# Mamba block of a four-layer graph network: chunks of 1, 2, 3, 4, 4, ... tiles, the graph convolution shared out by TensorE's load per slot, and gates, projections and exponentials in other slots

## The chip, the cores and the metric

One core of a Trainium2 chip runs the whole program. The time is the device time of one execution in microseconds (us), the median of several executions; the same kernel before the change is the base.

## The reference

Four layers work on 3327 rows of 256 numbers with a dense 3327 x 3327 matrix `adj`; each layer's result is added to its input and normalised by row. The change is all in the second layer, which is a graph convolution followed by a selective scan ("Mamba"):

```python
h = relu(adj @ x @ gcn_w + gcn_b)
h = layernorm(h) * ln_g + ln_b
xc, z = split(h @ w_in)                       # 512 channels each
u = silu(causal_conv4(xc) + conv_b)
dt_low, B, C = split(u @ w_xp)                # 16, 16 and 16 columns
dt = softplus(dt_low @ w_dt + b_dt)
# along the rows, for each of 512 channels and 16 states s:
state[s] = exp(dt * A[s]) * state[s] + dt * B[s] * u
y = sum_s(state[s] * C[s]) + u * D_skip
x = layernorm(x + (y * silu(z)) @ w_out)
```

The other layers are a graph layer (`adj @ x / degree`), a graph attention and a two-step nucleus attention. Their code is the same in both kernels.

## The kernel before

Rows are padded to 26 tiles of 128. A *chunk* is a run of tiles that the scan takes at once; before, the chunks have 2, 2, 3, 3, 4, 4, 4 and 4 tiles (list `ends`). Inside a chunk the kernel goes over the 16 states; one state of one chunk is a *slot*, written (c,s) here, and there are 128 of them. Channels lie on partitions in four groups `g`, rows along the free axis.

In slot k the engines do this, in the order of the loop over `states`:

- SP fetches the row pair (B, C) of slot k+2, broadcast over the partitions (`row`, three buffers).
- PE adds up the product of slot k-1 into PSUM by transposes (`add_up`).
- DVE does four scans (`scan`, one per group). Each needs `dA`, an exponential that ACT writes into one of two PSUM buffers (`decay`); ACT writes the third and fourth of this slot and the first two of the next one, each as soon as a scan has freed a buffer. Then DVE multiplies by C (`product`).
- ACT saves the last column (`carry`).
- POOL multiplies `du` by the B row of slot k+2 (`feed`), into the buffer that `product` has just read.
- After that come the slot's `uses`: on PE and ACT, work of the neighbouring chunks. For the chunk behind: `gated` and `residual` (slots 1 to 4) turn and project its output. For this chunk: `gate_input`. For the next chunk, the methods of class `Head`: `project` (which begins with a POOL copy of three columns, `t<-last`), `taps`, `silu`, `mixed`, `step_size`, `exponentials`, `logarithms`, `finish`, `skip`.
- Between the uses, `work_ahead` draws pieces of the graph convolution of later tiles from the generator `convolve`. A tile is 26 matmuls into one PSUM buffer `cb`, then a boundary: ACT copies `m`, PE transposes, ACT copies again, PE multiplies by `gcn_w`, ACT does the relu (`hn<-cb`), and only then is `cb` free. Three later steps (`measure`, `norm`, `turn`) normalise the tile and turn it into `hT`.

Before, a piece is 6 matmuls (`JM`), `quota` counts pieces and spreads them evenly in rows over the 16 slots, and half of a slot's pieces come between its first and its other uses. When all tiles are convolved, `work_ahead` calls `values`, which prepares the third layer's input tile by tile, as far as `ready` allows.

All these PSUM results of the uses share one buffer `ps`. From `pinned = True` on, class `Ordered` keeps every engine's instructions in the order in which the code issues them; they all have the line of that helper, L263. What stands before that point (the first tiles and the first `Head`) is ordered by the scheduler. So within an engine an instruction that waits holds up all that stand behind it.

Of the kernel before, what the change touches and what calls it, by code (L numbers as in the profile page):

```python
# [18 lines left out]
P = 128  # L19
# [2 lines left out]
JH = 13  # L22
J0 = 4
JC = 9
JM = 6
NS = 7
S0 = 5
WC = 512
DI = 512
NG = DI // P  # L30
# [16 lines left out]
def gnn_kernel(ctx: ExitStack, tc: tile.TileContext, n: int, a: dict, out: bass.AP):  # L47
# [109 lines left out]
    with tc.tile_pool(name="l1b", bufs=1) as wpool, tc.tile_pool(name="l1at", bufs=2) as l1at:  # L157
# [33 lines left out]
        with tc.tile_pool(name="l1aw", bufs=1) as cwork, tc.tile_pool(name="l1c", bufs=2) as ch, \  # L191
# [6 lines left out]
            def scratch():  # L198
                return tmp.tile([P, NG, 3 + WC], F32, name="t")
# [45 lines left out]
            ends = []  # L245
            while not ends or ends[-1] < npad:
                prev = ends[-1] if ends else 0
                ends.append(min(npad, prev + min(WC, (2 + len(ends) // 2) * P)))
            nch = len(ends)
            starts = [0] + ends[:-1]  # L250
            hTs, us, szs, rows_of = {}, {}, {}, {}
# [25 lines left out]
            def convolve():  # L277

                rest = []
                full = 0  # L280
                for it in range(nt):
                    cb = cpsum.tile([P, 2, D], F32, name="cb")
                    acc, tp = cb[:, 0, :], cb[:, 1, :]
                    for j in range(nt):
                        if j % JC == 0:
                            m = min(JC, nt - j)
                            at = l1at.tile([P, JC, P], F32, name="at")
                            nc.sync.dma_start(at[:, :m, :], a["adjT"][it][:, j:j + m, :])
                        ten.matmul(acc, at[:, j % JC, :], X0[:, j, :], start=(j == 0), stop=(j == nt - 1))
                        if j % JM == JM - 1 and j < nt - 1:  # L290
                            if rest:
                                rest.pop(0)()
                            yield full
                    m = cwork.tile([P, D], F32, name="m")
                    act.copy(m, acc)
                    while rest:
                        step = rest.pop(0)
                        step()
                        full += step is turn
                    yield full  # L300
                    for k in range(2):
                        ten.transpose(tp[:, k * P:(k + 1) * P], m[:, k * P:(k + 1) * P], ident)
                    mt = cwork.tile([P, D], F32, name="m")
                    act.copy(mt, tp)
                    yield full
# [4 lines left out]
                    act.activation(h, acc, AF.Relu)  # L310
# [12 lines left out]

                    def turn(it=it, h=h):
                        c = next(x for x in range(nch) if it * P < ends[x])
                        i = it * P - starts[c]
                        if i == 0:
                            hTs[c] = ch.tile([P, D // P, WC], F32, name="hT", bufs=3)
                        pt = psum.tile([P, WC], F32, name="ps")
                        for k in range(2):  # L330
                            ten.transpose(pt[:, k * P:(k + 1) * P], h[:, k * P:(k + 1) * P], ident)
                        for k in range(2):
                            act.activation(hTs[c][:, k, i:i + P], pt[:, k * P:(k + 1) * P], AF.Identity,
                                                 scale=g1[:, k:k + 1], bias=b1[:, k:k + 1])
                    rest = [lambda: None, measure, lambda: None, lambda: None, norm, turn]
                    while it == 0 and rest:
                        rest.pop(0)()
                    full += it == 0
                    yield full
                for step in rest[1:]:  # L340
                    step()
                    full += step is turn
                    yield full

            stream = convolve()
            done = taken = 0
# [2 lines left out]
            def advance():  # L349

                nonlocal done, taken
                t = next(stream, None)
                if t is not None:
                    done, taken = t, taken + 1
                return t is not None

            def pump(tiles):

                while done < min(tiles, nt) and advance():
                    pass  # L360

            def quota(c, s):


                c, s = divmod(c * DS + s + DS - S0, DS)
                t0 = ends[c] if c < nch else npad
                t1 = ends[c + 1] if c + 1 < nch else npad + P
                return max(0, math.ceil(NS * (t0 + (t1 - t0) * (s + 1) / DS) / P + NS - 1 - taken))

            def work_ahead(steps):  # L370

                for _ in range(steps):
                    if not advance():
                        return values()

            def value(it):

# [25 lines left out]
            class Head:  # L403
# [52 lines left out]
                    act.activation(self.v[:, g, :], ps[:, :w], AF.Identity, bias=b_dt[:, g:g + 1])  # L456
                    act.activation(self.e[:, g, :], ps[:, :w], AF.Abs, bias=b_dt[:, g:g + 1])

                def exponentials(self):

                    e = self.e
                    act.activation(e, e, AF.Exp, scale=-1.0)
                    self.e1 = scratch()[:, :, :self.w]
                    act.activation(self.e1, e, AF.Identity, bias=1.0)

                def logarithms(self):

# [106 lines left out]
                gps.tensor_scalar(nb, nb, -1.0, None, op0=ALU.mult)  # L574
                return rs, nb

            def tiles_of(c):
                return (ends[c] - starts[c]) // P

            pump(ends[0] // P)  # L580
            xs, ys = {}, {}
            first = Head(0)
            with tc.high_priority():
                for g in range(NG):
                    first.project(g)
                    first.taps(g)
            work_ahead(2)
            with tc.high_priority():
                first.silu()
                first.mixed()  # L590
            work_ahead(2)
            with tc.high_priority():
                for g in range(NG):
                    first.step_size(g)
            work_ahead(2)
            with tc.high_priority():
                first.exponentials()
                first.logarithms()
                first.finish()
                first.skip()  # L600
            states = [(c, s) for c in range(nch) for s in range(DS)]
            rows = {k: row(k) for k in range(2)}
            for k in range(2):
# [4 lines left out]
            for k, (c, s) in enumerate(states):  # L608
# [49 lines left out]
                if c and 1 <= s <= tiles_of(c - 1):  # L658
# [5 lines left out]
                    def projected(c=c, s=s, plus=plus, sums=sums):  # L664
                        sums[s] = residual(c - 1, s - 1, plus["gt"])
                    uses += [turned, projected]
                if s in (7, 8):
                    uses += [lambda i=i: gate_input(c, i) for i in range(2 * (s - 7), min(m, 2 * (s - 6)))]
                if after:
                    if s in (5, 6):  # L670
                        if s == S0:
                            pump(ends[c + 1] // P)
                        uses += [lambda g=g: ahead.project(g) for g in (2 * s - 10, 2 * s - 9)]
                    if s == 10:
                        uses += [ahead.mixed]
                    uses += [lambda g=g: ahead.step_size(g) for g in {10: (0,), 11: (1, 2), 12: (3,)}.get(s, ())]
                    if s == 12:
                        uses += [ahead.exponentials]
                    if s == 15:
                        uses += [ahead.skip]  # L680
                if c and s in (7, 8):
                    for i in range(2 * (s - 7), min(tiles_of(c - 1), 2 * (s - 6))):
                        x = X[:, starts[c - 1] // P + i, :]
                        rs, nb = plus["scales"]
                        act.activation(x, x, AF.Identity, scale=rs[:, i:i + 1], bias=nb[:, i:i + 1])
                    if s == 8:
                        ready = ends[c - 1] // P
# [835 lines left out]
```

## Time and profile before

| | us |
|---|---|
| median of three runs (3743.65 to 3745.7) | 3745.27 |
| the profiled execution: its time | 3741.57 |
| its span in the profile | 3739.6 |
| first layer and first convolved tiles, up to the first scan | 433.26 |
| slots (0,0) to (7,15), first scan to last scan | 1154.17 |
| of these, DVE busy | 898 |
| last scan to the third layer's start | 27.47 |

Times inside the profile are counted from the start of the span. The first scan of a slot marks its start. DVE's scans are the instructions `h<-dA,...`; `cb<-F,at` is a convolution matmul, which is two instructions on PE; `y<-ident,hc` is `add_up`. The granted clock is a share of TensorE's full clock.

### The profile page before, as it was taken

How to read it: one execution, taken by the hardware profiler on the slowest of the kernel's cores; microseconds unless marked ns; L12 is line 12 of the kernel's file. 1: busy time of each engine (PE TensorE's matmuls, PEld its weight loads, DVE VectorE, ACT ScalarE, POOL GpSimd, SP SyncE). 2: the span in 40 equal slices, each digit the busy share in tenths (PEclk: the TensorE clock that was granted, in tenths of full speed). 3: DMA queues.
4: the chain of work that ended last, by engine and by line, in shares of the span. 5: the costliest groups of instructions: out<-in, count | busy, mean ns of one | idle time of the engine just before them, and what ended most of it. 6: DMA issues, size and time to landing. Idle time of an engine off the chain costs nothing. (4 is left out here: it accounts for less than half of the span.)

```text
span 3739.6 us, 43358 instructions
## 1 busy us (share of the span) xinstructions
PE 3301.6 (88%) x15583; PEld 2604.1 (70%) x15583; DVE 2418.5 (65%) x5460; ACT 1705.0 (46%) x2594; POOL 903.5 (24%) x970
## 2 busy tenths in 40 slices
PE   9999787877877766589989999999999899999996
PEld 7888565665655645478876787787777677777775
DVE  1111377777888878867755445445442899999996
ACT  1000456455454555421113333333333888888883
POOL 0000143443544444511110000000000233333332
PEclk9999888888989887799999999999999999999998
DMA  7442333332323211234432221121121212222220
GB/s 243 138 138 97 93 92 85 89 96 79 105 86 87 77 48 51 51 118 144 151 109 60 63 61 53 57 63 52 56 64 53 65 56 66 66 66 66 66 62 22
DMA packets 151996, 308.01 MB, mean 82 GB/s; under 512 B 19859, under 2 KB 77395, under 8 KB 151635
## 3 DMA queue, kind: packets, MB, share of 16 engines
q1 hardware_dynamic: 151762, 305.06, 27.3%
q8 instruction: 126, 2.06, 0.2%
q14 instruction: 108, 0.88, 0.1%
HBM read 294.36 MB, written 10.65 MB: 82 GB/s over the span
## 5 line engine op out<-in xcount | busy, mean ns | idle before, releaser
L263 POOL TENSOR_TENSOR h<-du,row 128x2048 f32<-128x2048 f32 (+2 forms) x126 | 470.0, 3730 | 615.1 <-DVE hc L263 463.6
L263 DVE TENSOR_TENSOR_SCAN h<-dA,carry,h 128x512 f32<-128x512 f32 (+2 forms) x448 | 480.9, 1115 | 179.2 <-ACT dA L263 179.2
L263 ACT ACTIVATE dA<-t,A_log 128x512 f32<-128x512 f32 (+2 forms) x510 | 305.3, 609 | 276.8 <-DVE h L263 274.3
L263 PE MATMUL cb<-F,at 128*128 128x256 f32 x1148 | 296.4, 411 | 69.4 <-ACT hn L263 69.1
L966 PE MATMUL acc<-F,at 128*128 128x256 f32 x1352 | 352.5, 386 | 1.0 <-ACT q L740 0.6
L999 PE MATMUL acc<-X,wt 128*128 128x256 f32 x1352 | 343.6, 391 | 10.6 <-ACT wt L997 10.2
L999 PE MATMUL acc<-G,wt 128*128 128x256 f32 x1352 | 334.2, 390 | 5.7 <-ACT wt L930 5.3
L263 PE MATMUL y<-ident,hc 128*128 128x128 f32 x1648 | 253.3, 316 | 83.0 <-DVE hc L263 82.7
L263 PEld LDWEIGHTS cb<-F,at 128*128 128x128 f32 x1148 | 232.3, 207 | 133.0 <-ACT hn L263 77.2
L999 PEld LDWEIGHTS acc<-X,wt 128*128 128x128 f32 x1352 | 242.7, 190 | 105.3 <-issue 41.3
L119 PE MATMUL acc<-xa,at 128*128 128x257 f32 x1352 | 308.5, 381 | 5.9 <-DMA at<-in_adjT 5.7
L966 PE MATMUL acc<-X,at 128*128 128x256 f32 x1352 | 308.4, 381 | 0.0
L263 PEld LDWEIGHTS y<-ident,hc 128*128 128x128 f32 x1648 | 231.4, 166 | 110.1 <-DVE hc L263 97.1
L875 PE MATMUL acc<-F,at 128*128 128x257 f32 x1352 | 303.7, 381 | 1.1 <-ACT r L848 1.1
L999 PEld LDWEIGHTS acc<-G,wt 128*128 128x128 f32 x1352 | 248.8, 192 | 64.3 <-ACT wt L930 34.9
L1011 DVE MAX8 cand<-e 128x8 f32<-128x128 f32 x676 | 142.3, 279 | 228.8 <-ACT e L952 217.2
L966 PEld LDWEIGHTS acc<-F,at 128*128 128x128 f32 x1352 | 237.1, 190 | 74.9 <-issue 50.2
L119 PEld LDWEIGHTS acc<-xa,at 128*128 128x128 f32 x1352 | 255.6, 191 | 42.8 <-issue 6.2
L966 PEld LDWEIGHTS acc<-X,at 128*128 128x128 f32 x1352 | 253.0, 191 | 39.9 <-issue 8.0
L875 PEld LDWEIGHTS acc<-F,at 128*128 128x128 f32 x1352 | 253.6, 191 | 36.7 <-issue 1.3
L263 DVE TENSOR_TENSOR hc<-h,row 128x2048 f32<-128x2048 f32 (+2 forms) x128 | 243.7, 1904 | 10.3 <-PE y L263 4.2
L995 PE MATMUL tp<-ident,e 128*128 128x128 f32 x1352 | 196.6, 277 | 43.1 <-DVE e L1182 35.1
(361 smaller groups left out, 5150.7 us busy)
## 6 DMA issues: line engine op xcount, KB each, us to landing
at<-in_adjT SPq DMA_DIRECT2D x102, 832.0 KB, 4.4
at<-in_adjT SPq DMA_DIRECT2D x260, 320.0 KB, 2.9
row<-bc SPq DMA_DIRECT2D x64, 512.0 KB, 4.9
at<-in_adjT SPq DMA_DIRECT2D x52, 576.0 KB, 3.8
at<-in_adjT SPq DMA_DIRECT2D x26, 512.0 KB, 4.0
row<-bc SPq DMA_DIRECT2D x32, 384.0 KB, 4.8
row<-bc SPq DMA_DIRECT2D x32, 256.0 KB, 4.8
xt<-in_xT SPq DMA_DIRECT2D x26, 128.0 KB, 4.0
```

What stands on the lines that cost most here:

```text
L119: nc.tensor.matmul(acc, at[:, j, :], rhs[:, j0 + j, :], start=(j0 + j == 0), stop=(j0 + j == nt - 1))
L263: return lambda *x, **k: tc.keep_in_program_order(op(*x, **k))
L875: nc.tensor.matmul(acc, at[:, j, :], F[:, j0 + j, :], start=(j0 + j == 0), stop=(j0 + j == nt - 1))
L966: nc.tensor.matmul(acc, at[:, j, :], rhs[:, j0 + j, :], start=(j0 + j == 0), stop=(j0 + j == nt - 1))
L995: nc.tensor.transpose(pt[:, j, :], e[:, (j0 + j) * P:(j0 + j + 1) * P], ident)
L999: nc.tensor.matmul(acc, wt[:, j, :], rhs[:, j0 + j, :], start=(j0 + j == 0), stop=(j0 + j == nt - 1))
L1011: nc.vector.max(cand[:, s * 8:(s + 1) * 8], z[:, s * SEG:(s + 1) * SEG])
```

## The change

The chunks become 1, 2, 3, 4, 4, 4, 4 and 4 tiles. Convolution pieces become 3 matmuls, and each piece tells its load in units (4 for a 256-column matmul, so 122 for a tile with its boundary). `duty` gives the units that a slot's other work puts on PE, and `quota` fills the slots from slot 7 of one chunk to slot 6 of the next up to a common level, with a lead of `AHEAD` = 96 units. Between the first and the second use stands only what `SPLIT` leaves. `norm` and `turn` come two pieces later. The projections move from slots 5, 6 to slots 7, 8, the gates' inputs from 7, 8 to 5, 6, the taps from 7 (groups 0, 1), 8 (2) and 9 (3) to 8 (0, 1) and 9 (2, 3); the first half of the exponentials from slot 12 to slot 11; the scaling of the finished rows `X`, and with it `ready`, from slots 7, 8 to slot 14. Two tiles more than the first chunk are convolved before the loop.

```diff
-JM = 6
-NS = 7
-S0 = 5
+JM = 3
+TILE = 122
+AHEAD = 96
+SPLIT = 54
+S0 = 7
...
-                ends.append(min(npad, prev + min(WC, (2 + len(ends) // 2) * P)))
+                ends.append(min(npad, prev + min(WC, (1 + len(ends)) * P)))
...
                         if j % JM == JM - 1 and j < nt - 1:
                             if rest:
-                                rest.pop(0)()
-                            yield full
+                                step = rest.pop(0)
+                                step()
+                                full += step is turn
+                            yield full, 4 * JM
...
-                    rest = [lambda: None, measure, lambda: None, lambda: None, norm, turn]
-                    while it == 0 and rest:
-                        rest.pop(0)()
-                    full += it == 0
-                    yield full
+                    rest = [lambda: None, measure, *3 * [lambda: None], norm, lambda: None, turn]
+                    if not pinned:
+                        for step in (measure, norm, turn):
+                            step()
+                        rest = []
+                        full += 1
+                    yield full, 14
...
+            def duty(c, s):
+                if c >= nch:
+                    return 0
+                m, n, b = tiles_of(c), tiles_of(c + 1), tiles_of(c - 1)
+                return 4 * m * (2 if s == 0 else 1) + 20 * (1 <= s <= b) + 16 * len(gates(s, m)) \
+                    + 4 * n * len(projects(s)) + (8 * n if s == 10 else 0) + 2 * n * len(sizes(s))
...
             def quota(c, s):
                 c, s = divmod(c * DS + s + DS - S0, DS)
-                t0 = ends[c] if c < nch else npad
-                t1 = ends[c + 1] if c + 1 < nch else npad + P
-                return max(0, math.ceil(NS * (t0 + (t1 - t0) * (s + 1) / DS) / P + NS - 1 - taken))
+                if c not in shares:
+                    slots = [divmod((c - 1) * DS + S0 + i, DS) for i in range(DS)]
+                    busy = [duty(*x) for x in slots]
+                    more = TILE * tiles_of(c + 1)
+                    level = max(busy) + more
+                    while sum(max(0, level - x) for x in busy) > more:
+                        level -= 1
+                    shares[c] = [max(0, level - x) for x in busy]
+                target = TILE * ends[c] // P + sum(shares[c][:s + 1]) if c + 1 < nch else TILE * nt
+                return target + AHEAD - taken
...
-                def exponentials(self):
-                    e = self.e
+                def exponentials(self, g):
+                    e = self.e[:, g:g + 2, :]
                     act.activation(e, e, AF.Exp, scale=-1.0)
-                    self.e1 = scratch()[:, :, :self.w]
-                    act.activation(self.e1, e, AF.Identity, bias=1.0)
+                    if g:
+                        self.e1 = scratch()[:, :, :self.w]
+                        act.activation(self.e1, self.e, AF.Identity, bias=1.0)
...
-            work_ahead(2)
...
                 first.skip()
+            pump(ends[1] // P)
...
-                    for g in {7: (0, 1), 8: (2,), 9: (3,)}.get(s, ()):
+                    for g in {8: (0, 1), 9: (2, 3)}.get(s, ()):
                         ahead.taps(g)
...
-                if s in (7, 8):
-                    uses += [lambda i=i: gate_input(c, i) for i in range(2 * (s - 7), min(m, 2 * (s - 6)))]
+                uses += [lambda i=i: gate_input(c, i) for i in gates(s, m)]
                 if after:
-                    if s in (5, 6):
-                        if s == S0:
-                            pump(ends[c + 1] // P)
-                        uses += [lambda g=g: ahead.project(g) for g in (2 * s - 10, 2 * s - 9)]
+                    if s == S0:
+                        pump(ends[c + 1] // P)
+                    uses += [lambda g=g: ahead.project(g) for g in projects(s)]
...
-                    if s == 12:
-                        uses += [ahead.exponentials]
+                    if s in (11, 12):
+                        uses += [lambda: ahead.exponentials(2 * (s - 11))]
...
-                if c and s in (7, 8):
-                    for i in range(2 * (s - 7), min(tiles_of(c - 1), 2 * (s - 6))):
+                if c and s == 14:
+                    rs, nb = plus["scales"]
+                    for i in range(tiles_of(c - 1)):
...
-                q = quota(c, s) if done < nt else 2
+                q = quota(c, s)
+                if done == nt:
+                    for use in uses[:1]:
+                        use()
+                    values()
+                    for use in uses[1:]:
+                        use()
+                    values()
+                    continue
+                part = min(q, max(0, SPLIT - 4 * m - duty(c, s) // 2)) if len(uses) > 1 else q
                 for use in uses[:1]:
                     use()
-                work_ahead((q + 1) // 2)
+                work_ahead(part)
                 for use in uses[1:]:
                     use()
-                work_ahead(q // 2)
+                work_ahead(quota(c, s))
```

More of the change, by code (lines that the diff above doesn't have):

```diff
@@ L291, in convolve @@
                             if rest:
-                                rest.pop(0)()
-                            yield full
+                                step = rest.pop(0)
+                                step()
+                                full += step is turn
+                            yield full, 4 * JM
                     m = cwork.tile([P, D], F32, name="m")
                     act.copy(m, acc)
[L296 to L299, printed above, removed]
-                    yield full
+                    yield full, 8
                     for k in range(2):
@@ L304, in convolve @@
                     act.copy(mt, tp)
-                    yield full
+                    yield full, 4
                     for k in range(2):
@@ L334, in turn @@
                                                  scale=g1[:, k:k + 1], bias=b1[:, k:k + 1])
-                    rest = [lambda: None, measure, lambda: None, lambda: None, norm, turn]
-                    while it == 0 and rest:
-                        rest.pop(0)()
-                    full += it == 0
-                    yield full
+                    rest = [lambda: None, measure, *3 * [lambda: None], norm, lambda: None, turn]
[5 more added lines that the diff above has]
+                    yield full, 14
                 for step in rest[1:]:
@@ L342, in convolve @@
                     full += step is turn
-                    yield full
+                    yield full, 0
             stream = convolve()
@@ L353, in advance @@
                 if t is not None:
-                    done, taken = t, taken + 1
+                    done, taken = t[0], taken + t[1]
                 return t is not None
@@ L360, in pump, with tiles_of, gates, projects @@
                     pass
+            def duty(c, s):
[4 more added lines that the diff above has]
+                    + 4 * n * len(projects(s)) + (8 * n if s == 10 else 0) + 2 * n * len(sizes(s))
+            def tiles_of(c):
+                return (ends[c] - starts[c]) // P if 0 <= c < nch else 0
+            def gates(s, m):
+                return range(2 * (s - 5), min(m, 2 * (s - 4))) if s in (5, 6) else ()
+            def projects(s):
+                return range(2 * (s - S0), 2 * (s - S0) + 2) if s in (S0, S0 + 1) else ()
+            def sizes(s):
+                return {10: (0,), 11: (1, 2), 12: (3,)}.get(s, ())
+            shares = {}
             def quota(c, s):
                 c, s = divmod(c * DS + s + DS - S0, DS)
-                t0 = ends[c] if c < nch else npad
-                t1 = ends[c + 1] if c + 1 < nch else npad + P
-                return max(0, math.ceil(NS * (t0 + (t1 - t0) * (s + 1) / DS) / P + NS - 1 - taken))
-            def work_ahead(steps):
-                for _ in range(steps):
+                if c not in shares:
[8 more added lines that the diff above has]
+                return target + AHEAD - taken
+            def work_ahead(units):
+                while units > 0:
+                    before = taken
                     if not advance():
                         return values()
+                    units -= max(1, taken - before)
             def value(it):
@@ L575, in scales @@
                 return rs, nb
-            def tiles_of(c):
-                return (ends[c] - starts[c]) // P
             pump(ends[0] // P)
@@ L586, in gnn_kernel @@
                     first.taps(g)
-            work_ahead(2)
-            with tc.high_priority():
                 first.silu()
                 first.mixed()
-            work_ahead(2)
-            with tc.high_priority():
                 for g in range(NG):
                     first.step_size(g)
-            work_ahead(2)
-            with tc.high_priority():
-                first.exponentials()
+                for g in (0, 2):
+                    first.exponentials(g)
                 first.logarithms()
@@ L674, in gnn_kernel @@
                     if s == 10:
                         uses += [ahead.mixed]
-                    uses += [lambda g=g: ahead.step_size(g) for g in {10: (0,), 11: (1, 2), 12: (3,)}.get(s, ())]
-                    if s == 12:
-                        uses += [ahead.exponentials]
+                    uses += [lambda g=g: ahead.step_size(g) for g in sizes(s)]
+                    if s in (11, 12):
+                        uses += [lambda: ahead.exponentials(2 * (s - 11))]
                     if s == 15:
@@ L680, in gnn_kernel @@
                         uses += [ahead.skip]
-                if c and s in (7, 8):
-                    for i in range(2 * (s - 7), min(tiles_of(c - 1), 2 * (s - 6))):
+                if c and s == 14:
+                    rs, nb = plus["scales"]
+                    for i in range(tiles_of(c - 1)):
                         x = X[:, starts[c - 1] // P + i, :]
-                        rs, nb = plus["scales"]
                         act.activation(x, x, AF.Identity, scale=rs[:, i:i + 1], bias=nb[:, i:i + 1])
-                    if s == 8:
-                        ready = ends[c - 1] // P
@@ L688, in gnn_kernel @@
-                q = quota(c, s) if done < nt else 2
+                    ready = ends[c - 1] // P
+                q = quota(c, s)
[8 more added lines that the diff above has]
+                part = min(q, max(0, SPLIT - 4 * m - duty(c, s) // 2)) if len(uses) > 1 else q
                 for use in uses[:1]:
```

## Prediction

> **What bounds the kernel now.** I read the busy table by stretches first: one stretch from first scan to first scan of each chunk. Columns are length, then busy us of PE, PEld, DVE, ACT, POOL, the granted clock, DMA.
>
> ```profile
> 433.26:537.12 103.86, 81.09 (x361) 62.67 (x359) 70.71 (x102) 58.72 (x133) 41.83 (x27) 0.85 0.36 93
> 787.51:940.60 153.09, 119.82 (x532) 90.95 (x532) 111.63 (x118) 78.53 (x144) 62.78 (x33) 0.87 0.33 89
> 940.60:1108.81 168.21, 129.12 (x600) 99.17 (x600) 136.76 (x118) 86.40 (x146) 80.96 (x37) 0.88 0.32 93
> 1446.29:1587.43 141.14, 86.48 (x400) 69.22 (x400) 117.05 (x96) 66.84 (x138) 71.33 (x19) 0.78 0.21 52
> ```
>
> DVE is the fullest engine but idles 24 to 41 us in every chunk, whatever its size: 898 busy in 1154, so 256 us idle. The change can win only there, or before the first scan. Second, DVE's waits from 433 to 1587:
>
> ```profile
> DVE h L263 <- ACT dA L263: 201.0, 74, 7.2
> DVE X L263 <- PE ps L263: 28.4, 18, 3.4
> DVE sz L263 <- PE y L263: 6.0, 6, 1.8
> ```
>
> Four fifths is scans waiting for `dA`. ACT itself is half idle; it is late because its queue is in order and the uses in front of `dA` wait. Third, the timeline shows on what, in slots (4,5) and (4,6):
>
> ```profile
> 992.58 1.99 PE L263 MATMUL ps<-hT,w_in 128*128 128x512 f32 x4
> 992.77 2.45 DVE L263 TENSOR_TENSOR_SCAN h<-dA,carry,h 128x512 f32<-128x512 f32 x2
> 992.99 4.50 POOL L263 TENSOR_TENSOR h<-du,row 128x2048 f32<-128x2048 f32 x1 [2.58 <-DVE hc L263]
> 997.43 0.20 POOL L263 COPY t<-last 128x12 f32<-128x12 f32 x1
> 997.66 0.81 ACT L263 ACTIVATE u<-t,conv_b,conv_w 128x512 f32<-128x512 f32 x1 [5.86 <-POOL t L263]
> 998.38 0.36 ACT L263 ACTIVATE hn<-cb 128x256 f32<-128x256 f32 x1
> 998.64 0.58 ACT L263 COPY t<-ps 128x512 f32<-128x512 f32 x1
> 999.97 1.28 ACT L263 ACTIVATE dA<-t,A_log 128x512 f32<-128x512 f32 x2
> 1000.68 1.28 DVE L263 TENSOR_TENSOR_SCAN h<-dA,carry,h 128x512 f32<-128x512 f32 x1 [5.45 <-ACT dA L263]
> ```
>
> `project(0)` begins with a small POOL copy, queued behind the 4.5 us `feed`, which waits for this slot's product. So ACT's `u` stands until 4.9 us into the next slot, and the third scan waits 5.45 us.
>
> **The yardstick.** A plain 4-tile slot takes 7.10 us (slot (4,5)): scans to +4.90, product to +7.10. ACT is free for uses at about +5.6, and the next slot's third scan needs its `dA` at 7.10 + 2.46. With 0.7 for that `dA`, uses and their waits may last 3.2 us, plus any extra DVE work; what is longer is idle. I counted PE's instructions per slot in both programs at warm rates (16 transposes in 1.91, 24 convolution instructions in 5.36). Before, chunk 4's slots hold 2.0 to 11.1 us of PE work; after, 6.2 to 7.9. That part of the change does what it says. But waits of ACT on PE decide, not PE's sum, so I follow the order slot by slot.
>
> **1. Start of the scans: -24 us.** Before, PE runs all of tile 2 before the first projection:
>
> ```profile
> 386.81 11.52 PE L289 MATMUL cb<-F,at 128*128 128x256 f32 x52 [0.47 <-ACT hn L310]
> 399.50 1.13 PE L417 MATMUL ps<-hT,w_in 128*128 128x256 f32 x4 [0.27 <-ACT hT L333]
> 433.26 2.51 DVE L263 TENSOR_TENSOR_SCAN h<-dA,h 128x256 f32<-128x256 f32 x4 [2.53 <-POOL h L524]
> ```
>
> With a first chunk of one tile, the projection stands 7 matmuls into tile 1, near 375. The head's chain is then 128 columns wide and would allow a scan near 398. But tile 2's `bn_stats` precedes the first scan on DVE, so that scan waits for two whole tiles: from 373.5, 45 matmuls at 0.43 (19.4), two boundaries of 3.2 (m 383.21 to relu 386.38), and about 10 of the head's PE work and its waits, which stand between. That is 409, with 405 to 414 as bounds. One finished tile fewer is in hand, but PE has room for it in slots (0,0) to (0,6).
>
> **2. DVE's work: +2 us.** Same 26 x 16 tile-states. Plain slots take 7.01, 5.41 and 3.64 busy us for 4, 3 and 2 tiles, so about 1.9 for one tile. From the table by chunk: 43.5 + 79 + 110 + 136.8 + 2 x 138.4 + 137 + 117 = 900.
>
> **3. Idle of a 4-tile chunk with convolution: 32 us, as now (31.5 and 32.8).** The parts:
> - Slot 8 gets 11.5. The projections move to slot 7, with their POOL copy behind `feed` as before. And in every chunk a tile's boundary now lies between the two projections of slot 7: ACT's order is t, u, m, m, hn, t, u. After `u` (+5.6 into slot 8) come m to relu 3.2, the second projection 1.9 (it follows the boundary on PE), t 0.6, u 0.7, dA 0.7: third scan at +12.7, 10.2 idle. If PE is cold, 2 to 3 more. Today slots 6 and 7 idle 5.6 + 4.9 and slot 8 0.6; so this group goes from 11.1 to 13.3, with 1.8 in slot 7 for two gates and a turn.
> - Slots 11 to 13 get 9 (now 6.2 + 4.4 + 1.9, and 2.7 around them). `mixed` no longer waits behind 12 late convolution instructions, and 6 instead of 12 stand before the first step: slot 11 falls to 0 to 2.3. In slot 12 a whole boundary (ACT: m, m, hn) stands ahead of the exponentials, so slot 13 rises to 4.3 to 5.8, although half of one exponential is gone (1.0).
> - Slots 15 to 4 get 9 (now 5). In slot 15 the relu stands behind four `u*D_skip` (2.55) and `bn_stats` waits 1.5 for it; the 9 matmuls after it delay `add_up`, and the gates wait 1.4 to 3.7. The residuals wait about 1.7 in slot 2 (turn between) and 2.6 to 4.6 in slot 3 (boundary between).
> - Ordinary joints: 1.
>
> Moved at no cost: `taps` (slots 8 and 9 lengthen by 2.3 each, which covers their silus), and X's scaling in slot 14 (13.8 us long; its four copies, 2.1, fit the window). `at` loads still alternate with `row` fetches on SP. `measure` puts three small POOL instructions (1.3 together) behind `feed`, as before, and `norm` now asks for them two pieces later, so nothing new waits there.
>
> The clock is the widest unknown. After 7.55 us of rest PE did 12 convolution instructions in 4.92 us, and warm ones in 2.76:
>
> ```profile
> 1053.10 2.76 PE L263 MATMUL cb<-F,at 128*128 128x256 f32 x12
> 1087.71 4.92 PE L263 MATMUL cb<-F,at 128*128 128x256 f32 x12 [7.55 <-ACT hn L263]
> ```
>
> All of PE's pieces warm, the chunk idles 25; all cold that follow over 4 us of rest, 38. I take the middle, since rests of 4 to 8 us lie ahead of slots 8, 10 and 13 and none ahead of slots 1, 4 to 7.
>
> The Trainium skill, page "TensorE: Matmul & The Clock Gate", section "What's actually happening", says that the default is the throttled clock, and that one idle window of about 3.4 us brings it back. The rows here agree (3.44 us for 16 transposes after 4.33 idle, 1.97 after 1.32). By that rule a levelled PE that rests in the wrong places is punished, and the sum would be 38 a chunk, 18 us worse over three chunks; by a warm PE it would be 21 better.
>
> **4. The other chunks.** Chunk 0 (1 tile): 35. Its slots need 1.9 of DVE, but row fetch (4.0 to 4.8 landing) plus `feed` (half of 2.35) plus 0.3 serve two slots, so 2.95 each: 7 over slots 1 to 7; slot 0 2.3, slot 8 8.5 by the chain above with smaller tiles, 13 in slots 9 to 13 where 3 to 4.5 us of PE meet 1.9 to 3 of DVE, 4 at the end. Chunk 1: 32: slot 8 9.8, and slots 9 to 15 have 38 of PE and two boundaries (6.5) against 37 of DVE, 8; the rest 14. Chunk 2: 30. The first four chunks before idle 138 and hold the same ten tiles, against 129 here with one 4-tile chunk. Chunk 6: 36 (now 29.3): its slots 0 to 3 now carry convolution, +7. Chunk 7: 18 (now 24): gates and X's scaling no longer meet `values`.
>
> Sum: 35 + 32 + 30 + 3 x 32 + 36 + 18 = 247, against 256: **-9 us**.
>
> **5. The tail: +2.** `ready` comes in slot 14, so 6 tiles instead of 4 are left for `values` after the last scan. Each takes 3.9 us (1604.60 to 1608.49), but two can start in the 13 us before the first finished row.
>
> **Total.** -24 + 2 - 9 + 2 = -29 on the profiled 3741.6: 3712.6. The median is 3.7 above that execution: **3716**.
>
> **Rivals.** (a) *Levelling wins.* ACT's waits on PE go; slot 8 keeps only the old 5.6 and slots 11 to 13 nothing: 18 a chunk for seven chunks, about 84 less: 3632. For it: 201 us of DVE's idle hangs on ACT, and no slot keeps 10 us of PE work. Against: the order t, u, m, m, hn, t, u. 14%. (b) *Slower: the boundary between the projections.* It runs cold, and PE leaves slot 8 so late that the next slots start late. It decides once idle in 4-tile chunks passes 36 and in chunks 0 to 2 and 6 rises alike (29 us spread over seven chunks is 4 each); at 38, and 6 more in each of the other four, 42 us come back: 3758. 14%. (c) *The early start is given back.* Chunk 0, too short for its rows and for three tiles of convolution, idles 24 more (59): 3740, no change. 12%. My forecast, 3685 to 3737: 60%.
>
> **How the numbers follow.** A measurement of this kernel tells about 0.2% (7.5 us) from no change. Faster: forecast and (a), 74%; within: (c), 12%; slower: (b), 14%. The clock alone moves three chunks by 20 each way, the start by 5; below 3674 lie two thirds of (a), above 3752 two thirds of (b). Range 3674 to 3752.
>
> **What would show it.** Right: first scan near 409; in each chunk the longest DVE wait is slot 8's third scan, 10 to 13 us, behind ACT's second `u`; slot 11 under 3; slot 13 over 4; 4-tile chunks 165 to 173 long; granted clock in them 0.85 to 0.95. Wrong: 4-tile chunks near 150 mean (a), over 176 mean (b); a first scan after 420, or chunk 0 over 95 long, mean (c).

## The result and the profile after

The changed kernel takes 3759.05 us (median of 9) against 3745.7 for the kernel before (median of 9): ratio 1.0034, 95% interval 1.0023 to 1.0045. It is slower by a third of a per cent, which is the number of rival (b), 3758, and not my forecast of 3716. The profiled execution has a span of 3757.7 us, 18.2 more than before:

| | before, us | after, us | difference | forecast |
|---|---|---|---|---|
| first scan | 433.26 | 410.42 | -22.8 | -24 |
| DVE busy, first to last scan | 898.2 | 904.0 | +5.8 | +2 |
| DVE idle, first to last scan | 255.9 | 288.7 | +32.8 | -9 |
| last scan to the third layer | 27.5 | 30.6 | +3.1 | +2 |
| after that | 2124.7 | 2124.0 | -0.7 | 0 |

One row is far off, the idle time, which is the sum of terms 3 and 4. The same table by stretches as before (length, busy us of PE, PEld, DVE, ACT, POOL, clock), for chunks 0, 2, 4, 6 and 7:

```profile
410.42:491.25 80.83, 62.68 (x257) 47.02 (x258) 46.65 (x101) 46.20 (x122) 23.31 (x24) 0.83 0.26 76
610.81:761.56 150.75, 120.51 (x533) 88.28 (x532) 110.67 (x113) 78.41 (x142) 63.47 (x35) 0.88 0.33 89
932.47:1112.36 179.89, 138.77 (x616) 102.43 (x616) 138.09 (x121) 88.33 (x147) 82.27 (x35) 0.85 0.30 85
1291.47:1474.07 182.60, 113.30 (x506) 83.81 (x504) 137.10 (x116) 93.68 (x179) 76.97 (x28) 0.82 0.18 49
1474.07:1603.11 129.04, 78.46 (x378) 64.11 (x378) 116.75 (x96) 62.55 (x122) 70.65 (x19) 0.72 0.25 57
```

Length less the DVE column is idle time. The eight chunks have 34, 39, 40, 34, 42, 41, 45 and 12; I had said 35, 32, 30, 32, 32, 32, 36 and 18. DVE's waits over the whole stretch, again us in total, times, longest, say what kind of idle time it is:

```profile
DVE h L265 <- ACT dA L265: 186.7, 56, 13.8
DVE X L265 <- PE ps L265: 52.3, 16, 10.3
DVE sz L265 <- PE y L265: 17.5, 6, 4.0
DVE bnst L265 <- ACT hn L265: 15.5, 7, 4.3
```

The scans' waits for `dA` fell by 14 us and became fewer and longer. What rose are waits that I had priced as small change: `X` (the sum of `w_out`) from 28.4 to 52.3, the gates from 6.0 to 17.5, `bn_stats` from 5.8 to 15.5. The row of `bn_stats` before:

```profile
DVE bnst L263 <- ACT hn L263: 5.8, 1, 5.8
```

The longest wait for `dA` is, as foretold, slot 8's third scan. Slots (4,7) and (4,8):

```profile
1010.81 2.45 DVE L265 TENSOR_TENSOR_SCAN h<-dA,carry,h 128x512 f32<-128x512 f32 x2
1011.03 4.50 POOL L265 TENSOR_TENSOR h<-du,row 128x2048 f32<-128x2048 f32 x1 [2.56 <-issue]
1015.47 0.19 POOL L265 COPY t<-last 128x12 f32<-128x12 f32 x1
1015.70 0.81 ACT L265 ACTIVATE u<-t,conv_b,conv_w 128x512 f32<-128x512 f32 x1 [5.86 <-POOL t L265]
1016.42 0.35 ACT L265 COPY m<-cb 128x256 f32<-128x256 f32 x1
1016.83 0.69 PE L265 MATMUL cb<-ident,m 128*128 128x128 f32 x2 [7.69 <-ACT m L265]
1018.03 2.08 PE L265 MATMUL cb<-gcn_w,m 128*128 128x256 f32 x4 [0.52 <-ACT m L265]
1021.18 3.60 PE L265 MATMUL ps<-hT,w_in 128*128 128x512 f32 x4
1025.44 0.81 ACT L265 ACTIVATE u<-t,conv_b,conv_w 128x512 f32<-128x512 f32 x1
1026.87 2.46 DVE L265 TENSOR_TENSOR_SCAN h<-dA,carry,h 128x512 f32<-128x512 f32 x2 [13.60 <-ACT dA L265]
```

The bracket is idle time of that engine and who ended it. POOL's copy stands behind `feed`, ACT's `u` behind the copy, the boundary's `m` behind `u`, PE behind `m`; PE then computes boundary and second projection at half clock (*cold*: 2.08 us for `gcn_w` and 3.60 for the projection, where a run below has 1.13 and 1.98 at full clock, *warm*). The new price of `X` is seen in slots (4,2) and (4,3), and at its worst in (6,4):

```profile
963.25 0.69 PE L265 MATMUL cb<-ident,m 128*128 128x128 f32 x2 [3.13 <-ACT m L265]
967.61 3.78 PE L265 MATMUL ps<-w_out,gt 128*128 128x256 f32 x8
971.43 0.42 DVE L265 TENSOR_TENSOR X<-F,ps 128x256 f32<-128x256 f32 x1 [6.31 <-PE ps L265]
...
1341.29 0.60 ACT L265 ACTIVATE hn<-hn,nb,rs 128x256 f32<-128x256 f32 x1 [6.99 <-POOL nb L265]
1343.53 3.78 PE L265 MATMUL ps<-w_out,gt 128*128 128x256 f32 x8 [0.47 <-ACT hT L265]
1347.35 0.42 DVE L265 TENSOR_TENSOR X<-F,ps 128x256 f32<-128x256 f32 x1 [10.31 <-PE ps L265]
```

Among the uses of (4,2) a boundary stands between `gt` and `w_out`, and slot (4,3) waits for it. In (6,3) the last tile's remaining steps are issued in one go: `norm` waits for POOL, whose small instructions stand behind the 4.5 us `feed`, and `w_out` waits for the turn.

### The profile page after: what moved, and what is told of

It reads as the page before. It is cut to its first block, busy times and chain, and to the rows that moved or that the text cites. A ratio compares the mean times of both kernels' runs of the same rounds, so it can differ in the third digit from the quotient of the medians.

```text
span 3757.7 us, 43333 instructions
## 1 busy us (share of the span) xinstructions
PE 3329.9 (89%) x15583; PEld 2603.8 (69%) x15583; DVE 2420.3 (64%) x5460; ACT 1708.5 (45%) x2602; POOL 912.7 (24%) x970
## 3 DMA queue, kind: packets, MB, share of 16 engines
q8 instruction: 127, 2.08, 0.2%
## 5 line engine op out<-in xcount | busy, mean ns | idle before, releaser
L265 POOL TENSOR_TENSOR h<-du,row 128x2048 f32<-128x2048 f32 (+3 forms) x126 | 472.6, 3751 | 639.3 <-DVE hc L265 451.7
L265 DVE TENSOR_TENSOR_SCAN h<-dA,carry,h 128x512 f32<-128x512 f32 (+2 forms) x448 | 496.6, 1152 | 159.1 <-ACT dA L265 159.0
L265 ACT ACTIVATE dA<-t,A_log 128x512 f32<-128x512 f32 (+3 forms) x510 | 305.9, 610 | 305.9 <-DVE h L265 305.2
L1033 PE MATMUL acc<-X,wt 128*128 128x256 f32 x1352 | 345.3, 392 | 10.5 <-ACT wt L1031 10.3
L265 PE MATMUL cb<-F,at 128*128 128x256 f32 x1196 | 307.7, 409 | 13.5 <-ACT hn L265 13.5
L265 DVE TENSOR_TENSOR hc<-h,row 128x2048 f32<-128x2048 f32 (+3 forms) x128 | 245.6, 1918 | 7.1 <-issue 0.4
L1031 ACT COPY wt<-tp 128x512 f32<-128x512 f32 (+1 forms) x182 | 93.6, 557 | 311.4 <-PE tp L1029 311.3
```

The costliest lines, as they stand in the source:

```text
L265: return lambda *x, **k: tc.keep_in_program_order(op(*x, **k))
L1031: copy(wt[:, :m, :], pt[:, :m, :])
L1033: nc.tensor.matmul(acc, wt[:, j, :], rhs[:, j0 + j, :], start=(j0 + j == 0), stop=(j0 + j == nt - 1))
```

## The experiments

Each ratio is to runs of the kernel before on the same chip, with its 95% interval. Differences in us from the changed kernel are from its 3759; the kernel before took 3744.7 to 3745.9 in every group of runs. "Slot 8" is DVE's idle time in that slot in chunks 4 and 5, 13.7 to 13.9 us in the changed kernel.

### What slot 8 is made of

**Copy first.** `t<-last` is issued in slot 7 ahead of `feed`.

```diff
+                if after and s == S0:
+                    ahead.carried()          # gps.tensor_copy(self.xc[:, :, :3], last)
                 if k + 2 < len(states):
                     feed(k + 2)
```

> The changed kernel with one move: GpSimd's copy of the three carried columns (t<-last) is issued ahead of slot 7's feed instead of behind it. My theory (GpSimd's 4.5 us feed holds ACT's first u by 5.9 us, ACT's queue holds the boundary's m behind it, TensorE rests 7.7 us and then computes boundary and second projection cold): slot 8's idle time falls from 13 to 14 us to some 6 to 8 us in chunks 1 to 5, and the run comes 30 to 45 us under the changed kernel's 3759. Rival 'cold clock alone' (the rest after the boundary's m is long enough to cool TensorE whatever the copy does, and the copy is hidden): 0 to -10 us. Rival 'first chunks' (the loss is in the smaller first chunks or in the levelled convolution): no change.

3732.7 us, ratio 0.9971 (0.9958 to 0.9983), 26 under the changed kernel. Slot 8: 8.0 and 7.6. ACT's 5.86 us wait is gone, and the boundary starts after 1.92 us of rest. But it still runs cold:

```profile
996.51 0.55 PE L265 MATMUL cb<-ident,m 128*128 128x128 f32 x2 [1.92 <-ACT m L265]
997.57 2.08 PE L265 MATMUL cb<-gcn_w,m 128*128 128x256 f32 x4 [0.52 <-ACT m L265]
1000.72 3.78 PE L265 MATMUL ps<-hT,w_in 128*128 128x512 f32 x4
```

The gain is just under my 30 to 45: slot 8 gave 34 us over the seven chunks, and 7 of them came back in other slots.

**Boundary last.** Convolution between two uses stops ahead of a boundary.

```diff
-                while units > 0:
+                while units > 0 and (whole or taken % TILE < 96):
...
-                work_ahead(part)
+                work_ahead(part, len(uses) < 2)
```

> The changed kernel, but the convolution that stands between two uses of a slot stops ahead of a tile's boundary (last two matmuls, copy, transposes, gcn_w, w_dt, hn), so that in slot 7 both projections and in slots 1 to 4 w_out come before it; GpSimd's copy stays behind the feed. My theory: ACT's first u still waits for the copy, but the second u no longer waits for a boundary; the boundary's own chain on ACT then stands ahead of slot 8's exps instead, so slot 8 keeps about 9 to 10 of its 13.7 us, slot 3 gives back 2 to 3 of its 6.4 us; in all 20 to 40 us under the changed kernel. Rival 'it is the copy alone': 0 to -8 us. Rival 'first chunks': no change.

3745.5 us, 1.0006 (0.9996 to 1.0016): 14 under the changed kernel, level with the kernel before, below the 20 to 40 expected. Slot 8 is 10.5, slot 3 4.6 in place of 6.4; slot 12 of chunks 1 and 2, where the boundary now meets the exponentials, rose from 8 to 11.

**Both.**

> Both moves: the copy ahead of the feed, and no boundary between two uses. My theory: slot 8's idle time is 4 to 7 us, slot 3's 3 to 5 us, and the run is 45 to 70 us under the changed kernel (3690 to 3715), so under the kernel before as well. Rival 'cold clock alone': -10 to -25 us. Rival 'first chunks': no change, 3755 to 3762.

3711.1 us, 0.9916 (0.9902 to 0.9931). Slot 8 is 4.3: PE now rests 0.92 us before the transposes and the boundary is warm:

```profile
990.97 0.44 PE L265 MATMUL cb<-ident,m 128*128 128x128 f32 x2 [0.92 <-ACT m L265]
991.92 1.13 PE L265 MATMUL cb<-gcn_w,m 128*128 128x256 f32 x4 [0.52 <-ACT m L265]
```

**The clock by itself.** Matmuls that nobody reads fill PE's rest ahead of the boundary in slot 7.

```diff
+                    if hot:                  # only in slot S0, between the projections
+                        dm = psum.tile([P, WC], F32, name="ps")
+                        for k in range(30):  # second run: 15
+                            ten.matmul(dm[:, :D], ident, gw[:, 0, :], start=True, stop=True)
                     for k in range(2):
                         ten.transpose(tp[:, k * P:(k + 1) * P], m[:, k * P:(k + 1) * P], ident)
```

> The changed kernel with 30 more matmuls of 128x256 into a PSUM tile that nobody reads, on TensorE's queue where it rests 7.7 us ahead of the boundary's transposes in slot 7; every other instruction as in the changed kernel, so ACT waits for GpSimd's copy as long as before. It tells the cold clock from the wait. My theory: both count; with TensorE kept busy the transposes, gcn_w, w_dt and the second projection take 0.44, 1.03, 0.69 and 1.9 us in place of 0.69, 2.08, 1.22 and 3.6, so slot 8 loses 3 to 4 of its 13.7 idle us: 18 to 28 us under 3759. Rival 'the wait alone': within 5 us of 3759. Rival 'the clock alone': slot 8 idle under 6 us, 50 us or more under.

3783.0 us, 1.0096 (1.0081 to 1.0111): slower, a miss of mine. 30 calls are 60 instructions and took 13.2 us, so they outlasted the rest. The second run fits it:

> As the run with 30 more matmuls ahead of the boundary in slot 7, but with 15: each is two instructions, so 30 took 13.2 us, more than the 7.7 us of rest, and held the boundary up by 6.3 us, for which slot 8 idled only 2.8 us longer (16.5 against 13.7). 15 take 6.6 us and fit into the rest. My theory (clock and wait both count): slot 8 idles 10 to 11 us in place of 13.7, 15 to 25 us in all: 3734 to 3744. Rival 'the wait alone': 3755 to 3762.

3748.4 us, 1.0008 (0.9999 to 1.0017), 11 under the changed kernel, slot 8 10.4. ACT waits for the copy as long as before; only the clock differs:

```profile
1004.95 6.74 PE L265 MATMUL ps<-gcn_w,ident 128*128 128x256 f32 x30 [0.76 <-ACT t L265]
1010.78 0.81 ACT L265 ACTIVATE u<-t,conv_b,conv_w 128x512 f32<-128x512 f32 x1 [5.88 <-POOL t L265]
1012.86 1.13 PE L265 MATMUL cb<-gcn_w,m 128*128 128x256 f32 x4 [0.52 <-ACT m L265]
1014.54 1.98 PE L265 MATMUL ps<-hT,w_in 128*128 128x512 f32 x4
1018.61 1.28 DVE L265 TENSOR_TENSOR_SCAN h<-dA,carry,h 128x512 f32<-128x512 f32 x1 [10.29 <-ACT dA L265]
```

So of slot 8's 13.8 us, POOL's copy is worth 5.8, the cold clock 3.4 and the boundary's place 3.3, each taken away alone. They overlap and do not simply add: the run with both moves, which is rid of all three, still has 4.3. The 15 to 25 us expected came out as 11: slot 8 gave 3.4 in chunks 3 to 5, 0.8 to 2.7 in the smaller ones, and none in chunk 6, where no convolution is left in slot 7.

### Was it in the kernel before as well?

**The kernel before, copy first**, the same move in its slot 5.

> The kernel before with GpSimd's copy of the carried columns ahead of the feed of slot 5, and nothing else. My theory: the wait for that copy stood in the kernel before as well (slots 6 and 7 idle for 5.6 and 4.9 us in its 4-tile chunks, behind ACT's first u of slot 5): 2 to 5 us go in each of seven chunks, 14 to 35 us under 3745. Rival 'only the new order made it cost' (in the kernel before something else ends slot 6's wait): 0 to -7 us.

3714.5 us, 0.992 (0.9905 to 0.9934): 31 us, more than the same move gives the changed kernel. So POOL's copy is the largest single loss in slot 8 and yet no reason why the changed kernel is the slower one: both had it.

**The kernel before with the new chunks alone** (`(1 + len(ends)) * P` for `(2 + len(ends) // 2) * P`).

> The kernel before with the new list of chunks (1,2,3,4,4,4,4,4 tiles in place of 2,2,3,3,4,4,4,4) and nothing else. My theory: the list by itself is not what costs; the scans start about 24 us earlier, one 16-slot joint more or less costs nothing, and the small first chunks cost at most half of it back in idle time: 3715 to 3740 against 3745. Rival 'first chunks': the early start is given back whole or more, 3745 to 3760.

3748.2 us, 1.0013 (1.0004 to 1.0022). My range missed: the first scan comes at 399.68, 34 us earlier, and nothing is won. Chunk 0 idles 58.7 us; slot (0,0) alone lasts 20.3 us, because DVE's `bn_stats` of tile 2 waits behind its 26 matmuls. DVE's waits in chunk 0:

```profile
DVE h L263 <- ACT dA L263: 32.3, 9, 5.1
DVE bnst L263 <- ACT hn L263: 16.8, 2, 15.7
```

**Both moves, old chunks.**

> The kernel with both moves (copy ahead of the feed, no boundary between two uses: 3711 us) with the old list of chunks 2,2,3,3,4,4,4,4. The list by itself gave nothing on the kernel before (3748 against 3745.5), since that kernel's first slot then had 17 us of convolution to wait for. My theory: here, with the second chunk's tiles done ahead of the scans, the early start counts: the old list starts its scans some 20 us later and costs 12 to 30 us: 3723 to 3741. Rival 'the list gives nothing here either' (the short slots of a chunk of one tile give the start back): 3705 to 3715.

3716.4 us, 0.9924 (0.9911 to 0.9937), against 0.9916: the list is worth some 5 us, which the two intervals do not tell from nothing. The scans start 19.4 us later, but chunks 0 to 3 take 488.2 us in place of 500.5. Here the rival, that the early start is given back, held for two thirds of it.

### DVE's waits for X

**`w_out` straight behind `gt`** in slots 1 to 4.

```diff
+                if c and 1 <= s <= tiles_of(c - 1):
+                    part = 0
```

> The changed kernel, but in the slots that turn and project a gated tile (slots 1 to 4) w_out comes straight behind gt, and all of the slot's convolution behind it; nothing else is changed. Against the kernel before, DVE's waits for dA fell from 201 to 187 us, but those for X (w_out's sum) rose from 28 to 52. My theory: most of that rise is the turn or the boundary that stands between gt and w_out; X's waits fall by 15 to 25 us, slot 8 is untouched, and the run comes 10 to 25 us under 3759. Rival 'given back': the convolution that is put off holds up the next slot's exps and products by as much, and the run stays within 5 us of 3759.

3743.9 us, 0.9995 (0.9985 to 1.0005): 15 under the changed kernel, level with the kernel before, with slot 8 untouched. DVE's waits:

```profile
DVE h L265 <- ACT dA L265: 210.0, 63, 13.8
DVE X L265 <- PE ps L265: 9.0, 12, 2.3
```

`X` gives back 43 us and `dA` takes 23 of them. As good a repair as taking the boundary out from between the uses, with which it overlaps: that run's waits for `X` had fallen by 14 us too.

**The last tile's steps one per half slot.**

```diff
                 while units > 0:
+                    if taken == TILE * nt:
+                        advance()
+                        return
                     before = taken
```

> The changed kernel, but once the last tile is convolved its remaining steps (measure, norm, turn) are issued one per half slot instead of all in slot (6,3), where w_out stood behind the turn and VectorE waited 10.3 us for X in slot (6,4). My theory: slot (6,4)'s 11.4 idle us fall to 1 to 3 and come back nowhere: 8 to 11 us under 3759. Rival 'given back' (chunk 6's later slots or the first projection of chunk 7 wait for the later turn): 0 to -4 us.

3749.5 us, 1.0013 (1.0003 to 1.0023): 10 under. Slot (6,4) falls from 11.4 to 0.6 us.

### The boundary inside the next slot

**Copy first, last tile spread, and the boundary taken apart**, so that its copies stand behind the exps that DVE waits for (its three steps are due at 96, 104 and 108 of a tile's 122 units).

```diff
-                while units > 0:
+                while units > 0 and (taken % TILE < 96 or not pinned):
...
                     elif k + 1 < len(states):
                         dAs.append(decay(k + 1, g - 2))
+                    if taken % TILE == {0: 96, 1: 104, 3: 108}.get(g):
+                        advance()
```

> The changed kernel with the copy ahead of the feed and the boundary taken apart: the convolution stops ahead of a boundary, and in the next slot its three steps are issued behind that slot's exps (last matmuls and m behind the third exp, transposes and second m behind the fourth, gcn_w, w_dt and hn behind the next slot's second exp), so that none of ACT's boundary copies stands ahead of an exp that VectorE waits for; after the last tile one step a half slot. My theory (what is left in the kernel with both moves is ACT's fixed order: m, m and hn in front of the next exps, 4 to 6 us in slots 3, 8 and 13 each): idle time of a 4-tile chunk falls from 32 to some 17 to 24 us, 40 to 75 us under 3711: 3636 to 3671. Rival 'the work itself' (TensorE's load of the slot, cold where it now rests at the end of a slot, sets the end whatever the order): 3690 to 3715.

3652.5 us, 0.9752 (0.9739 to 0.9764): 107 us under the changed kernel, 2.5% under the kernel before, the fastest of all runs. Chunk 4 is 160.3 us long with 22 idle:

```profile
891.43:1051.69 160.26, 130.25 (x618) 98.37 (x617) 138.29 (x122) 88.48 (x148) 82.42 (x35) 0.91 0.36 96
```

DVE's waits from first to last scan, against 186.7 and 52.3 in the changed kernel:

```profile
DVE h L265 <- ACT dA L265: 128.4, 74, 6.3
DVE X L265 <- PE ps L265: 29.0, 16, 3.6
```

**The same in the kernel before** (copy first, transposes behind the fourth exp, `gcn_w` to `hn` behind the next slot's second; `{1: 5, 3: 6}` of its 7 pieces).

> The kernel before (old chunks, even convolution, projections in slots 5 and 6) with the copy ahead of the feed (3714 us by itself) and with the boundary's transposes and its gcn_w, w_dt and hn issued in the next slot behind the fourth exp and behind the next slot's second exp. It asks what the change's new slots and levelled convolution are worth once both kernels are free of the two waits: the changed kernel came to 3652 so. My theory: the boundary's place in ACT's queue cost the kernel before too (slots 11 and 12 idle 6 and 4.4 us), 25 to 50 us: 3665 to 3690, so 10 to 35 us remain for the change's own moves. Rival 'the gain rests on the levelled convolution': 3705 to 3716. Rival 'the moves are worth nothing': 3645 to 3658.

3690.4 us, 0.9856 (0.9841 to 0.9871). This is just past the 3665 to 3690 expected. Freed of much the same waits in both (here the boundary's last matmuls and first copy stay where they were), the change is worth 38 us. It earns 26 at the start, 13 in the first ten tiles and 13 in the last two chunks, and gives 15 back in chunks 4 and 5; chunk 4 is 152.0 us here, 8 shorter than in the changed order.

**Old slots** for projections (5, 6), taps and gates' inputs (7, 8), all else as in the 3652 us kernel.

> The changed kernel with copy first and boundary inside the next slot (3652 us), with the projections back in slots 5 and 6, the taps in slots 7, 8 and 9 and the gates' inputs in slots 7 and 8 as in the kernel before; the chunks, the levelled convolution and the exps in two halves stay. My theory (the slots themselves matter little, the order inside them does): 3644 to 3662. Rival 'the new slots carry the gain': 3670 to 3690. Rival 'the new slots cost': under 3640.

3669.2 us, 0.9801 (0.9788 to 0.9814): the new slots are worth 17 us, more than I thought and less than the rival.

**`w_out` forward and `X` behind the second scan** (`work_ahead(part, 84)`; `if g == 1 and s - 1 in sums`).

> The same 3652 us kernel with w_out brought forward: the convolution between gt and w_out stops ahead of the last tile's turn as well (ACT's two hT copies held w_out up in slot 2), and VectorE adds w_out's sum to X behind the slot's second scan in place of its first (and measures it behind the third). My theory: VectorE's waits for that sum (3.5 us in slot 2 and 2.8 us in slot 3 of a 4-tile chunk) fall by 2 us or so each, 10 to 25 us in all: 3627 to 3643. Rival 'another wait takes their place' (the scans' exps, TensorE's products): 3648 to 3656.

3657.0 us, 0.9768 (0.9754 to 0.9782): nothing won, the rival held. `X` fell from 29.0 to 2.7 us and `dA` rose from 128.4 to 150.6; slot 12 of chunks 4 and 5 went from 2.7 to 5.9, slot 0 from 0.7 to 2.2.

### Is it the levelling?

Since the kernel before with both moves has the shorter 4-tile chunks, I suspected the levelled shares. The edit makes them even:

```diff
-                    level = max(busy) + more
-                    while sum(max(0, level - x) for x in busy) > more:
-                        level -= 1
-                    shares[c] = [max(0, level - x) for x in busy]
+                    shares[c] = [more // DS] * DS
```

> The 3652 us kernel (copy first, boundary inside the next slot) with the convolution's shares made even, 30 units in each of the 16 slots of a 4-tile chunk, in place of levelled by TensorE's load; chunks, slots and pieces as there. The kernel before with both moves, whose convolution is even, runs a 4-tile chunk in 152.0 us with 15.3 idle, against 160.3 and 22.0 here. My theory: the levelling itself costs (it fills the slots with light load, whose length DVE's 7.1 us sets and where ACT has the least room): 4-tile chunks of 152 to 156, 3620 to 3640. Rival 'the levelling is neutral' (the slots or the pieces of 3 make the difference): 3647 to 3658. Rival 'the levelling helps': 3660 or more.

> The same with projections back in slots 5 and 6 and gates' inputs in 7 and 8 (3669 us when levelled). My theory: the levelling costs here too, 4-tile chunks of 152 to 156 in place of 160.5: 3632 to 3655. Rival 'the levelling is neutral': 3664 to 3674.

> The changed kernel itself, without either move, with even shares. If the levelling costs by itself, 15 to 35 us under 3759 (3724 to 3744). If it only shifts where the boundaries fall, the sign is open and the run stays within 12 us of 3759.

The first took 3678.6 us (0.9818, 0.9804 to 0.9831), the second 3664.1 (0.9786, 0.977 to 0.9803), the third 3782.2 (1.0093, 1.0078 to 1.0109). My suspicion fell. With the new slots the levelling is worth 23 us in the changed kernel and 26 in the 3652 us one; with the old slots it makes no difference that these intervals can tell (3664 and 3669). Chunk 4 stays at 160.7 with even shares (13 us of the gain lie in chunks 1 to 3, the rest in several pieces of under 5) and at 158.3 with even shares and old slots. Why a 4-tile chunk is 6 to 9 us longer than in the repaired kernel before stays open. Untried of what still differs: pieces of 3 matmuls, the exponentials in two halves, the scaling of `X` in slot 14, the place of `norm` and `turn`. (Counted in matmuls these two come earlier than before, not later: after 18 and 24 of the next tile, where the old order had both behind its 26.)

## Why the prediction was wrong

**Term 1, start, right**: 410.42 where I said 409, for the reason given (`bn_stats` of tile 2, at 409.86, stands just ahead of it on DVE). **Term 2, work, small**: +5.8 for +2; chunk 0 is 46.7 busy, not 43.5. **Term 5, tail**: +3.1 for +2.

**Term 3, the idle time of a 4-tile chunk, failed at the step "I take the middle"** between 25 and 38. Chunks 4 and 5 idle 41.8 and 41.0, beyond the cold end, and chunk 3 idles 34.4. That is 21 us more than three times 32; another 21 are term 4's. In chunk 4, by my groups: slots 7 and 8 15.7 (13.3 said, 11.1 before); slots 11 to 13 10.4 (9 said, 12.5 before); slots 15 to 4 14.9 (9 said, 5 before). The order t, u, m, m, hn, t, u and the wait behind POOL's copy were read rightly and slot 11 is 1.5, as said; the worst sizing was in slots 15 to 4, where I had the turn and the boundary between `gt` and `w_out`, but at warm durations (slot 3 2.6 to 4.6, measured 6.4) and for slot 2 half of the price (1.7, measured 3.6). Clock and order are not two independent costs: a queue that waits makes PE rest, the rest makes PE cold, and the cold PE lengthens the very chain that is waited for. The levelled shares, which my sum gave no price of their own, are worth 23 us here.

**Term 4** failed in chunks 1 and 2 (39 and 40 for 32 and 30; slot 12 alone idles 8, where I had spread two boundaries over slots 9 to 15) and in chunk 6 (45 for 36: the last tile's steps in slot (6,3) cost 10, and I did not see them). Chunk 0 was right (34 for 35), and chunk 7 gave 6 back (12 for 18).

**Rival (b)** hit the number (3758) and its threshold (over 36 idle), by the place only in part: slot 8 came out 2.3 us over my figure; the rest came from `X` and the gates, and slots 9 and 10 do not start late (0.2 and 0.1 idle). Nor did chunk 0 rise. So the exact hit is in part luck. **Rival (a)**, levelling wins, fails on the ACT order, as argued against it. Its 84 us do not come out of 18 a chunk in seven chunks either: that is 126 if 18 is the gain, 103 if 18 stay idle. **Rival (c)** was wrong in place (chunk 0 idles 34, not 59) but right in kind: in the kernel before, the list alone gained nothing.

The Trainium skill's clock gate ("TensorE: Matmul & The Clock Gate", "What's actually happening") describes free-running windows of about 3.4 us. The trace agrees with the length: in stretches of 3.41 us the clock column reads whole ones and halves,

```profile
1010.81:1014.22 3.41, 0.00 (x0) 0.00 (x0) 2.45 (x3) 0.00 (x0) 3.19 (x1) 1.00 0.69 248
1014.22:1017.63 3.41, 0.69 (x2) 0.29 (x2) 0.00 (x0) 1.09 (x3) 1.45 (x2) 0.50 0.17 52
1017.63:1021.05 3.42, 3.02 (x6) 1.67 (x6) 0.00 (x0) 0.35 (x1) 0.00 (x0) 0.50 0.00 0
1021.05:1024.46 3.41, 3.41 (x5) 1.41 (x5) 0.00 (x0) 0.38 (x1) 0.00 (x0) 0.50 0.00 0
```

One window with no PE work is followed by three at half clock. But a window with PE work can be followed by them too, as the last section shows, so the idle window of the prediction's rule is not needed, and the measurement decides. The price of the cold clock is the measured one: 3.4 us in slot 8.

## What to carry to other kernels

In engines with fixed order, price each use by the whole chain of instructions it stands in front of, on every queue it crosses; a 0.2 us copy behind a 4.5 us multiply cost 26 to 31 us in each kernel. Put copies that serve later work behind the instruction that the bottleneck engine waits for, not ahead of it: three steps placed so, with that copy and the last tile's steps spread, turned 3759 into 3652. When one wait is removed, look at which wait takes its place before counting the gain (`X` gave 43 us and `dA` took 23; later 26 and 22).

## What the runs showed of the hardware

- PE need not rest for a whole window to lose its clock. In the run with the copy first, a stretch with 1.49 us of PE work in 3.41 was followed by three at half clock, two of them with PE busy throughout:

```profile
993.29:996.70 3.41, 1.49 (x8) 0.80 (x6) 3.32 (x3) 2.59 (x6) 0.82 (x5) 1.00 0.32 54
996.70:1000.11 3.41, 2.89 (x7) 1.68 (x7) 2.02 (x2) 0.37 (x1) 3.41 (x1) 0.50 0.67 230
1000.11:1003.53 3.42, 3.42 (x6) 1.26 (x5) 0.00 (x0) 0.38 (x1) 0.88 (x1) 0.50 0.14 43
1003.53:1006.94 3.41, 3.41 (x15) 2.79 (x14) 0.35 (x1) 2.37 (x4) 0.00 (x0) 0.50 0.00 0
```

  PE's busy time in a stretch does not tell by itself what follows. In the changed kernel 1.40 us of it kept the full clock and 2.53 us lost it:

```profile
1031.29:1034.70 3.41, 1.40 (x4) 0.33 (x2) 3.34 (x5) 1.61 (x3) 0.00 (x0) 1.00 0.00 0
1034.70:1038.11 3.41, 2.07 (x18) 2.05 (x19) 3.41 (x3) 0.69 (x1) 1.99 (x1) 1.00 0.17 55
1068.84:1072.25 3.41, 2.53 (x10) 1.15 (x8) 3.32 (x3) 2.18 (x5) 0.00 (x0) 1.00 0.00 0
1072.25:1075.66 3.41, 1.57 (x4) 1.08 (x5) 3.41 (x3) 1.65 (x4) 1.89 (x1) 0.50 0.78 220
```

- Work that nobody reads can pay: 6.7 us of it, filling PE's rest ahead of a boundary, kept PE warm and took 11 us off the run; 13.2 us, more than the rest, added 24.
- An f32 matmul call of 256 columns is two instructions on PE; 30 calls took 13.2 us.
